# A decoder layer on one Trainium2 core: one unit's operand splits placed elsewhere, and seven steps of the passage to the feed-forward part reordered

## The chip, the cores and the metric

The kernel runs on one core of one Trainium2 chip. A core has five engines that run their own instruction streams side by side: TensorE (PE in the profile; its weight loads are PEld), VectorE (DVE), ScalarE (ACT), GpSimd (POOL) and SyncE (SP, which here only issues transfers). The metric is the device time of one execution in microseconds (us); smaller is better. The kernel before was run three times: 1386.6, 1388.0 and 1388.14 us, median 1388.0.

## What is computed

A post-norm decoder layer over 8 sequences of 256 tokens of 512 features (2048 tokens, 16 tiles of 128): a causal self-attention with 16 heads of 128 and rotary positions, a cross-attention with 16 heads of 32 over a context of the same size, and a feed-forward part of 2048 features with both products quantized (inputs to 8 bits per token, weights to three values). Cut to what matters:

```python
# self-attention: 16 heads x 128, rotary q and k, causal (masked scores are 0, not -inf)
scores = where(causal, q @ k.T / sqrt(128), 0)
m = max(abs(scores)); sgn = sign(scores)
attn_w = sgn * exp(sgn * scores - m)
attn = attn_w / (sum(abs(attn_w)) + 1e-6)
x = layernorm(x + (attn @ v) @ W_O + b_O)
# cross-attention, its result scaled and normalized
probs = softmax(clip(where(mask, q2 @ k2.T / sqrt(32), -1e4), -50, 50))
delta = rs * ((probs @ v2) @ Wo.T + bo)
x = layernorm(x + (delta - mean) / sqrt(var + EPS) * ln_gamma + ln_beta)
# feed-forward: bitlinear(x, w, b) = quant8(x) @ ternary(w).T + b
scale = 127 / max(abs(x), EPS)          # per token, in quant8
h = layernorm(gelu(bitlinear(x, w1, b1))) * gamma + beta
x = layernorm(x + bitlinear(h, w2, b2))
```

## The kernel before, in words

**Self-attention.** The work is cut into 32 units: 8 pairs of heads (hp) by 4 pairs of sequences (bp), the sequences inside. A unit projects q, k and v, turns q and k by the rotary tables, makes scores, exponentials, transposed weights, the product with v and the output projection. Most products need more than one pass: an fp32 operand is split into a high part (hi, a cast to fp32r) and the rest (lo), and `mm3` (L145 to L148) adds hi·hi (L146), hi·lo (L147) and lo·hi (L148). So whatever TensorE reads is split first: a cast and a subtraction, in `split` (L155 to L157) both at once, in `half_split` (L181 to L187) one at a time: L185 is the cast on ScalarE, L183 the subtraction. Units with hp 0 split their own input `xt` from two loaded halves (`raw`, three buffers). Unit 2's first half is split by `xsplit(0)`, its second by two calls of `x_half`; `xload` issues the two loads of a unit.

The order within a unit is a string of two- and three-letter words, `SCHED["unit"]` (L60 to L71). A word is a method with its indices: Q projects, s scores, a takes their magnitude and sign (L385, L386), S masks, m takes the maximum (L397, L398), x exponentials (L406), n the sum's reciprocal (L411, L412), N multiplies weight, reciprocal and sign into e (L419), t transposes e on TensorE (L426), c and k split it (L432, L433, L439), z multiplies with v (L146 to L148, L449), y and l split the result (L453, L458), o projects it (`ppo`). For q and k: w swaps halves (L314, L315), u multiplies with the cosine (L320), r with the sine (L324 on POOL), R adds (L330, L332 on POOL), H casts to hi (L341), L subtracts (L347 and L348). A unit's projections run interleaved with the attention of the unit before and the output projection of the one before that. Words such as X0, XA, XB, BY, G1 and BW are places at which `background` (L522 to L611) puts extra pieces: the next unit's splits, loads, and weights. For unit 1, whose neighbours have little to interleave, the string is altered by a list of replacements (L633 to L637). ScalarE, VectorE, POOL and SP are held to the order written; TensorE's order in these units is left to the framework's scheduler.

**The rest** (cross-attention, the quantized inputs, the feed-forward part) is written as steps `S(...)` (L686) with the tiles that they read and write. A planner (L1234 to L1348) simulates the engines, picks by priorities from a table (`PLAN`), and writes the steps into the list `done`; where a step may run on two engines, a string in `PLAN` says which. The steps are then emitted in the order of `done`, and all five engines are held to that order.

For each of the 16 token tiles, unit ("x", b) ends with the second norm and the quantized input of the feed-forward part: `rstd` (L764, L765 on POOL) makes the reciprocal deviation, L980 the normalized row, `absmax` (L985 to L987) the quantization scale, `inverse` (L992 to L1001, POOL) the factor `a1s` and three bf16 pieces of the reciprocal, put into `xq[:, 512:640]` beside the quantized values (L1004, L1008). L1006 adds the bias b2 to the row, on POOL or VectorE. SP then transposes `xq` (L1010) and stores it (L1011). A feed-forward tile f loads it (L1060), multiplies with the first weights (L1070, L1071), Gelu on ScalarE (L1075), mean (L1080), squares (L1084, ScalarE), `spread` (L1089 to L1091, POOL), the norm with gamma and beta in two halves (L1095, L1108 on VectorE for one; L1103 on ScalarE, L1105 on VectorE and L1107 on POOL for the other), the maximum (L1111), the scale (L1116 to L1118; L1121 on POOL), the quantization (L1124 on ScalarE, L1125 on VectorE), SP's transposing transfer of `hq` to `hT` (L1153), the second product (L1131, L1133), the sum (L1155), the last norm (L753, L754, L764, L765, L768) and its row y (L1161), and the store (L1162). SP issues its transfers one after the other, in order, and waits at each for its source.

Of the kernel before, what the change touches and what calls it, by code (L numbers as in the profile page):

```python
# [11 lines left out]
F32R = mybir.dt.float32r  # L12
# [4 lines left out]
ALU = mybir.AluOpType  # L17
AX = mybir.AxisListType

B, S, D = 8, 256, 512  # L20
# [4 lines left out]
NT = NTOK // 128  # L25
# [7 lines left out]
EPS = 1e-5  # L33
# [45 lines left out]
def decoder_kernel(ctx: ExitStack, tc: tile.TileContext, a, out):  # L79
    nc = tc.nc  # L80
# [27 lines left out]
    def T(tag, shape, dt=F32, name=None):  # L108
        return (keep if tag in ("w", "xt") else sb).tile(shape, dt, name=name or tag, tag=tag, bufs=BUFS.get(tag, 1))
# [66 lines left out]
    def x_half(t, raw, i, part, eng):  # L176
        tf = t.rearrange("p h k c -> p h (k c)")
        cs = slice(1024 * i, 1024 * i + 1024)
        half_split(tf[:, 0, cs], tf[:, 1, cs], raw, part, eng)
# [342 lines left out]
    def background(ui):  # L522
        u = units[ui]
        ex = {k: [] for k in ("B0", "BA", "BV", "BW", "BX", "BY", "XA", "XB", "X0", "X1", "G0", "G1", "BP", "WK", "WV")}
        if ui == 0:
            ex["WK"].append(lambda: load_first("wK"))
            ex["WV"].append(lambda: load_hp(0, "wV", first["wV"]))
        nx = units[ui + 1] if ui + 1 < len(units) else None
        if nx is not None and nx.hp == 0:
            if ui == 0:  # L530
                ex["BA"].append(nx.xload)
            ex["X0" if ui < 2 else "B0"].append(lambda: nx.xsplit(0))
            ex["XA"].append(lambda: x_half(nx.xt, nx.raws[1], 1, 0, nc.scalar))
            ex["XB" if ui > 1 else "X1"].append(lambda: x_half(nx.xt, nx.raws[1], 1, 1, nc.vector))
        elif nx is not None:
            ex["BA"].append(nx.load)
        if ui < 2:
            ex["BV" if ui else "BW"].append(units[ui + 2].xload)
        if u.hp == 0:
            ex["BA" if ui else "X1"].append(lambda: init_acc(u.bp))  # L540
            ex["BA" if ui else "X1"].append(lambda: nc.sync.dma_start(f32(xs[u.bp][:]), f32(u.xt[:])))
        if "wv" in late:
            ex["B0"].append(lambda raw=late.pop("wv"): load_hp(u.hp, "wV", raw["w"]))
        for n, hp, k1 in ([("wO", u.hp, "BW")] if ui else [], [] if ui > 1 else [("wO", 0, "BW")], [("wQ", u.hp + 1, "BW")], [("wK", u.hp + 1, ""), ("wV", u.hp + 1, "")])[u.bp]:
            if (ui or n == "wO") and hp < NHP:
                raws = {}
                ex["BV" if n == "wV" else "BA"].append(lambda n=n, hp=hp, raws=raws: raws.update(w=raw_load(a[n][hp])))
                if n == "wV":
                    late["wv"] = raws
                elif n == "wK":  # L550
                    def hi(raws=raws, hp=hp):
                        w = hw.setdefault(hp, {})["wK"] = T("w", [128, 2, 1024], F32R)
                        half_split(w[:, 0], w[:, 1], raws["w"], 0, nc.scalar)

                    def lo(raws=raws, hp=hp):
                        w = hw[hp]["wK"]
                        half_split(w[:, 0], w[:, 1], raws["w"], 1, nc.vector)

                    ex["G0"].append(hi)
                    ex["BX"].append(lo)  # L560
                else:
                    ex[k1].append(lambda n=n, hp=hp, raws=raws: load_hp(hp, n, raws["w"]))
        if ui in ABS:
            for j in range(2):
                i, rr = 2 * ABS.index(ui) + j, {}
                ex["BA"].append(lambda i=i, rr=rr: rr.update(w=wchunk(i // 8, i % 8)))
                ex[f"G{j}"].append(lambda i=i, rr=rr: wq_abs(rr["w"], i // 8, i % 8))
        if "r2" in late:
            ex["B0"].append(lambda f=late.pop("r2"): run(f))
        for n, ci in enumerate(ROUND.get(ui, ())):  # L570
            cr = {}
            ex["BV" if n else "BA"].append(lambda cr=cr, ci=ci: cr.update(w=wchunk(ci // 8, ci % 8)))
            fs = [lambda step=step, cr=cr, ci=ci: wq_round(cr["w"], ci // 8, ci % 8, step) for step in range(3)]
            if n:
                late["r2"] = fs
            else:
                for k, f in zip(("G0", "G1", "BW"), fs):
                    ex[k].append(f)
        if ui == 1:
            ex["BA"].append(lambda: bo.update(t=bcast("bc", "bO")))  # L580
        if ui == len(units) - 2:
            ex["BA"].append(lambda: kv0.update(wk0r=raw_load(a["wkx"][:, 0:1024])))
            ex["BW"].append(lambda: kv0.update(wk0=split_w(kv0["wk0r"])))
        if ui == len(units) - 1:
            ex["BA"].append(lambda: kv0.update(cr=x_raws(a["ctxT"][0])))

            def ctx_split(i):
                if i == 0:
                    kv0["ctx"] = T("xt", [128, 2, 4, 512], F32R)
                x_split(kv0["ctx"], kv0["cr"][i], i, (nc.vector, nc.gpsimd)[i])  # L590

            ex["X0"].append(lambda: ctx_split(0))
            ex["X0"].append(lambda: kv0.update(wk1r=raw_load(a["wkx"][:, 1024:2048])))

            def last(part, e):
                if part == 0:
                    kv0["wk1"] = T("w", [128, 2, 1024], F32R)
                x_half(kv0["ctx"], kv0["cr"][1], 1, part, e)
                half_split(kv0["wk1"][:, 0], kv0["wk1"][:, 1], kv0["wk1r"], part, e)

            ex["G0"].append(lambda: last(0, nc.scalar))
            ex["BW"].append(lambda: last(1, nc.vector))
        if ui == 4:
            ex["BA"].append(setup_late)
        if ui == 5:
            ex["G0"].append(setup_late2)
        if ui in (A0 + 8, A0 + 9):
            ex["G0"] += [lambda wi=wi: (wq_tot, wq_mean)[ui - A0 - 8](wi) for wi in range(2)]
        if A0 + 2 <= ui < A0 + 18:
            ex["BP"].append(lambda: add_bo(ui - A0 - 2))  # L610
        return ex  # L611
# [19 lines left out]
    for ui, u in enumerate(units):  # L631
        spec = SCHED["unit" if ui else "first"]
        if ui == 1:  # L633
            for old, new in ((" N0 XB", ""), (" n0 m1", " n0 N0 m1"), ("Q000 s00 Q001", "Q000 Q001 s00"), (" S0 BA", " S0 BA f0- f2-"),
                             (" V0 v0", ""), (" t00", " V0 v0 t00")):
                assert old in spec
                spec = spec.replace(old, new, 1)  # L637
        emit(spec, u, units[ui - 1] if ui > 0 else None, units[ui - 2] if ui > 1 else None, background(ui))
        if ui == 0:
            in_order(["PE", "Activation", "DVE", "Pool", "SP"])  # L640
# [120 lines left out]
        nc.scalar.activation(mv[:, 1:2], mv[:, 6:7], AF.Identity, scale=1.0 / D)  # L761

    def rstd(mv):
        nc.gpsimd.tensor_scalar(mv[:, 2:3], mv[:, 1:2], EPS, None, ALU.add)  # L764
        nc.gpsimd.tensor_tensor(mv[:, 3:4], mv[:, 2:3], nhalf, ALU.pow)  # L765

    def shift(mv):
# [86 lines left out]
    def x(b):  # L854
# [80 lines left out]
        for qi in range(2):  # L935
# [29 lines left out]
            def scale1(m1=m1):  # L965
# [9 lines left out]
              rd=[m1, A], wr=[d])  # L975
            S([("DVE", 0.8, lambda d=d, m2=m2: stats(H[d], H[m2])),
               ("ACT", 2.1, lambda d=d, m2=m2, xq=xq: astats(H[d], H[m2], H[xq][:, 0:512]))], rd=[d], wr=[m2, f"{xq}/q"], new=[m2] + new(xq))
            S([("POOL-", 1.0, lambda m2=m2: rstd(H[m2]))], wr=[m2])
            S([("DVE", 0.13, lambda m2=m2: shift(H[m2]))], wr=[m2])
            S([("ACT", 0.71, lambda tt=tt, d=d, m2=m2: nc.scalar.activation(acc[:, tt], H[d], AF.Identity, bias=H[m2][:, 2:3], scale=H[m2][:, 3:4]))],  # L980
              rd=[d, m2], wr=[A])
# [8 lines left out]

            def inverse(tt=tt, m2=m2, xq=xq):
                s, xq = H[m2], H[xq]  # L992
                nc.gpsimd.tensor_tensor(a1s[:, tt : tt + 1], s[:, 10:11], wscale[:, 0:1], ALU.mult)
                nc.gpsimd.memset(xq[:, 512:640], 0.0)
                inv = s[:, 12:13]
                nc.gpsimd.tensor_tensor(inv, s[:, 11:12], wscale[:, 2:3], ALU.mult)
                for n in (3, 2, 1):
                    c0 = 512 + 33 * (3 - n)
                    nc.gpsimd.tensor_copy(xq[:, c0 : c0 + 32 * n - 31 : 32], inv.to_broadcast([128, n]))
                    if n > 1:  # L1000
                        nc.gpsimd.tensor_tensor(inv, inv, xq[:, c0 : c0 + 1], ALU.subtract)  # L1001
# [293 lines left out]
    while pool_:  # L1295
# [47 lines left out]
        for t in succ[s]:  # L1343
            need[t] -= 1
            ready[t] = max(ready[t], end + LAG[s.eng] if s in t.deps else now)
            if need[t] == 0:
                insort(pool_, t, key=lambda s: (s.prio, s.i))
    assert len(done) == len(steps)  # L1348
    for s in done:
        for k in s.new:  # L1350
            g = place[k]
            p = px[g] if g in px else keep if g in ("w", "xt") else post
            H[k] = p.tile(tiles[k][1], tiles[k][2], name=k, tag=g, bufs=CAP[g])
        s.fn()
# [70 lines left out]
```

## Time and profile before

| | |
|---|---|
| median of three runs | 1388.0 us |
| profiled execution | 1387.89 us |
| its span, first to last instruction | 1386.1 us |
| around the span | 1.8 us |
| granted TensorE clock, mean | 0.992 |
| TensorE busy | 1346.7 us (97%) |
| VectorE busy | 1091.8 us (79%) |
| ScalarE busy | 880.4 us (64%) |
| POOL busy | 782.0 us (56%) |

Times in the profile are microseconds from the start of the span. A row names the line of the kernel, the operation, the tile written and those read. `xt` is a unit's split input, `raw` a loaded piece, `u` the rotated operand, `rh` its split parts, `ppj` a projection in PSUM, `pwt` transposed weights, `ppo` the output projection; `xq`, `xT` and `xqs` the quantized input, its transpose and its place in DRAM; `up` and `dn` the two feed-forward products, `h` the hidden row, `fs` its statistics, `hq` and `hT` its quantized form and that one's transpose, `mb` the statistics of the second norm and `my` those of the last. Self-attention ends at about 905 us, cross-attention at about 1230; the feed-forward part overlaps its end and runs on to 1386. A row's duration includes what the instruction waits for inside the engine, so the same instruction can show different durations.

In the waits, the columns after the colon are us in total, times, and the longest. In the chain of waits they are start, duration and what it was. In the timeline they are start, duration, engine, line, operation, tiles and shapes; idle time before an instruction and what ended it stand in brackets.

### The profile page before, as it was taken

What the parts mean: (1) busy time and instruction counts of PE and PEld (TensorE: products, weight loads), DVE (VectorE), ACT (ScalarE), POOL (GpSimd) and SP (SyncE); (2) the same over time, 40 slices, a digit from 0 to 9 for tenths busy, and PEclk for the clock granted to TensorE, in tenths of its full rate; (3) what the DMA queues carried; (4) which work ended last, traced back from release to release, by engine and by line L of the source; (5) the groups of instructions that cost most, each with busy time, mean ns of one, the idle gap of its engine ahead of it and who ended that gap; (6) DMA issues with size and microseconds to landing.
All of it is one profiled execution on the core that took longest, in us unless ns stands there. A gap on an engine that the chain in (4) does not pass through costs nothing.

```text
span 1386.1 us, 23778 instructions
## 1 busy us (share of the span) xinstructions
PE 1346.7 (97%) x8576; PEld 1081.0 (78%) x8576; DVE 1091.8 (79%) x2040; ACT 880.4 (64%) x1948; POOL 782.0 (56%) x985
## 2 busy tenths in 40 slices
PE   9899999999999999999999999999999999988896
PEld 7789988898889888998889888888667667543342
DVE  6877768778767888887877876868767877798997
ACT  4666776776776666666665666633644445576995
POOL 5656556656666666766665665525033324376764
PEclk9999999999999999999999999999999999999999
DMA  8442342234322244223422342225324424214453
GB/s 309 182 185 109 116 178 107 92 114 165 121 76 96 92 143 176 104 84 124 189 88 99 126 175 107 69 99 191 114 59 126 140 68 143 86 34 94 113 116 99
DMA packets 85046, 170.13 MB, mean 123 GB/s; under 512 B 47040, under 2 KB 57024, under 8 KB 80064
## 3 DMA queue, kind: packets, MB, share of 16 engines
q1 hardware_dynamic: 82624, 165.99, 35.1%
q10 hardware_dynamic: 2304, 2.62, 0.7%
q8 instruction: 68, 1.11, 0.3%
q14 instruction: 50, 0.41, 0.1%
HBM read 130.31 MB, written 27.79 MB: 114 GB/s over the span
## 4 chain that ended last, share of the span: by engine, by line
PE 82%; DVE 10%; POOL 3%; ACT 2%; issue 2%; DMA 1%; SPq 0%; POOLq 0%; ACTq 0%; DVEq 0%
PE ppj L146 12%; PE ppj L147 12%; PE ppj L148 12%; PE pz L146 3%; PE pz L148 3%; PE pz L147 3%; PE pwt L426 3%; PE sc L880 3%; PE den L911 2%; PE av L895 2%; PE ppo L146 2%; PE ppo L147 2%; PE ppo L148 2%; PE psc L376 2%; PE pz L449 2%
## 5 line engine op out<-in xcount | busy, mean ns | idle before, releaser
L324 POOL TENSOR_TENSOR sw<-sw,stab 128x512 f32<-128x512 f32 x128 | 170.2, 1329 | 101.5 <-ACT sw L315 101.0
L146 PE MATMUL ppj<-xt,w 128*128 128x512 f32 x528 | 209.0, 396 | 0.3 <-ACT xt L285 0.3
L147 PE MATMUL ppj<-xt,w 128*128 128x512 f32 x528 | 206.5, 391 | 1.0 <-DVE xt L157 0.4
L148 PE MATMUL ppj<-xt,w 128*128 128x512 f32 x528 | 206.2, 391 | 0.0
L146 PE MATMUL ppj<-w,xt 128*128 128x256 f32 (+1 forms) x528 | 157.2, 298 | 1.1 <-DVE u L320 1.1
L348 POOL TENSOR_TENSOR rh<-u,rh 128x512 fp32r<-128x512 f32 x64 | 97.6, 1526 | 99.8 <-PE ppj L148 88.2
L148 PE MATMUL ppj<-w,xt 128*128 128x256 f32 (+1 forms) x528 | 152.0, 288 | 0.0
L147 PE MATMUL ppj<-w,xt 128*128 128x256 f32 (+1 forms) x528 | 151.9, 288 | 0.0
L320 DVE SCALAR_TENSOR_TENSOR u<-ppj,bqk,ctab 128x512 f32<-128x512 f32 x128 | 95.5, 746 | 70.9 <-ACT sw L315 70.6
L314 ACT ACTIVATE sw<-ppj,bqk 64x512 f32<-64x512 f32 x128 | 87.8, 686 | 92.7 <-PE ppj L148 87.9
L332 POOL TENSOR_TENSOR u<-u,sw 128x256 f32<-128x256 f32 (+1 forms) x128 | 130.8, 1022 | 0.3 <-DVE u L320 0.2
L419 DVE SCALAR_TENSOR_TENSOR e<-aw,rd,sg 128x128 f32<-128x128 f32 (+1 forms) x256 | 126.3, 550 | 0.1
L148 PEld LDWEIGHTS ppj<-xt,w 128*128 128x128 f32 x528 | 99.2, 188 | 21.6 <-DVE w L183 0.4
L406 ACT ACTIVATE aw<-aw,nm 128x256 f32<-128x256 f32 (+1 forms) x256 | 113.2, 443 | 3.9 <-DVE nm L397 3.9
L391 POOL TENSOR_SCALAR_AFFINE_SELECT aw<-aw 128x256 f32<-128x256 f32 x128 | 59.9, 492 | 98.7 <-ACT aw L385 98.7
L453 ACT CAST z<-pz 128x512 fp32r<-128x512 f32 x64 | 37.6, 587 | 121.3 <-PE pz L449 121.3
L147 PEld LDWEIGHTS ppj<-xt,w 128*128 128x128 f32 x528 | 99.3, 188 | 17.9 <-DVE xt L183 0.8
L146 PEld LDWEIGHTS ppj<-xt,w 128*128 128x128 f32 x528 | 99.3, 188 | 17.1 <-ACT xt L285 0.7
L146 PEld LDWEIGHTS ppj<-w,xt 128*128 128x128 f32 x528 | 101.9, 193 | 2.0 <-DVE u L320 1.4
L147 PEld LDWEIGHTS ppj<-w,xt 128*128 128x128 f32 x528 | 102.0, 193 | 0.6
L148 PEld LDWEIGHTS ppj<-w,xt 128*128 128x128 f32 x528 | 101.7, 193 | 0.7
L385 ACT ACTIVATE aw<-psc 128x384 f32<-128x384 f32 x128 | 62.3, 487 | 60.6 <-PE psc L148 59.9
(283 smaller groups left out, 3937.0 us busy)
## 6 DMA issues: line engine op xcount, KB each, us to landing
xt<-xs SPq DMA_DIRECT2D x28, 2048.0 KB, 8.2
xs<-xt SPq DMA_DIRECT2D x4, 2048.0 KB, 12.9
raw<-w1T SPq DMA_DIRECT2D x16, 512.0 KB, 9.5
raw<-w2T SPq DMA_DIRECT2D x16, 512.0 KB, 9.6
acc<-xn SPq DMA_DIRECT2D x4, 1024.0 KB, 8.5
raw<-wO SPq DMA_DIRECT2D x8, 512.0 KB, 9.6
wq<-wqt SPq DMA_DIRECT2D x16, 256.0 KB, 2.4
kx<-ks SPq DMA_DIRECT2D x8, 512.0 KB, 4.9
```

The costliest lines, as they stand in the source:

```text
L146: nc.tensor.matmul(ps, lh, rh, start=first, stop=False)
L147: nc.tensor.matmul(ps, lh, rl, start=False, stop=False)
L148: nc.tensor.matmul(ps, ll, rh, start=False, stop=last)
L314: nc.scalar.activation(sw[0:64], ps[64:128], AF.Identity, bias=bias[64:128])
L320: nc.vector.scalar_tensor_tensor(v3(u), v3(self.ps.pop((h, i))), self.bias(h, i), ctab.to_broadcast([128, 2, 256]), ALU.add, ALU.mult)
L324: nc.gpsimd.tensor_tensor(v3(sw), v3(sw), stab.to_broadcast([128, 2, 256]), ALU.mult)
L332: nc.gpsimd.tensor_tensor(u, u, sw, ALU.add)
L348: (nc.gpsimd if i else nc.vector).tensor_tensor(lo, u if i else u[:, :, 128:256], f32(hi), ALU.subtract)
L385: nc.scalar.activation(aw[:, h], sc3, AF.Abs, scale=1.0 / math.sqrt(DH))
L391: nc.gpsimd.affine_select(aw[:, :, blk], aw[:, :, blk], pattern=[[0, 2], [-1, 128]], compare_op=ALU.is_ge, fill=MASKED, base=0, channel_mu ...
L406: nc.scalar.activation(aw[:, h, blk], aw[:, h, blk], AF.Exp, bias=nm[:, h, i : i + 1], accum_out=rd[:, h, i : i + 1])
L419: nc.vector.scalar_tensor_tensor(e[:, h, blk], aw[:, h, blk], rd[:, h, i : i + 1], sg[:, h, blk], ALU.mult, ALU.mult)
```

## The change

**Unit 1.** The first half of unit 2's input is split after the second block's e (`N1 X0`), not after the first block's maxima. Its second half's hi (ScalarE, `XA`) comes just before `l0`, its lo (VectorE) at `BY`. The first block's sum and e (`n0 N0`) come right before the second half of the key's `L00`, `u10` and `m1`; `x0` comes before `H00`. The weight wO of the first head pair is split in two steps, hi on ScalarE at `G1` and lo on VectorE at `BW`, where it was cast and subtracted on VectorE at `BW`.

**rstd** multiplies by 1.0 and adds EPS in one instruction, where it added EPS alone.

**inverse** makes `a1s` and the reciprocal for tiles 0 to 14 by one product of two columns, the reciprocal in the next column of `a1s`; the last tile keeps two products. The memset of `xq[:, 512:640]` moves to the step of the second norm's `rstd`.

**Seven steps** are moved by hand in `done` after the planner: hT0's transfer ahead of the transposition of xT14; tile 3's squares (L1084) ahead of tile 2's first quantization (L1124); behind both beta products (L1107) of tiles 2 and 1, and ahead of L1121 of tile 0, in this order: tile 3's `spread`, the last tile's `inverse`, and the last L1006, which also goes from VectorE to POOL; and xT15's transposition and store behind the first output store, ahead of hT3's transfer. SP's order was: xT14, xT15, their two stores, hT0, hT1, hT2, the first output, hT3. It is: hT0, xT14, its store, hT1, hT2, the first output, xT15, its store, hT3.

```diff
@@ background @@
-            ex["XB" if ui > 1 else "X1"].append(lambda: x_half(nx.xt, nx.raws[1], 1, 1, nc.vector))
+            ex["XB" if ui > 1 else "BY" if ui else "X1"].append(lambda: x_half(nx.xt, nx.raws[1], 1, 1, nc.vector))
...
-                elif n == "wK":
-                    def hi(raws=raws, hp=hp):
-                        w = hw.setdefault(hp, {})["wK"] = T("w", [128, 2, 1024], F32R)
+                elif n == "wK" or ui == 1:
+                    def hi(raws=raws, hp=hp, n=n):
+                        w = hw.setdefault(hp, {})[n] = T("w", [128, 2, 1024], F32R)
                         half_split(w[:, 0], w[:, 1], raws["w"], 0, nc.scalar)
...
-                    ex["G0"].append(hi)
-                    ex["BX"].append(lo)
+                    ex["G0" if n == "wK" else "G1"].append(hi)
+                    ex["BX" if n == "wK" else "BW"].append(lo)
@@ the order of unit 1 @@
-            for old, new in ((" N0 XB", ""), (" n0 m1", " n0 N0 m1"), ("Q000 s00 Q001", "Q000 Q001 s00"), (" S0 BA", " S0 BA f0- f2-"),
+            for old, new in ((" N0 XB", ""), (" L00 n0 m1", " n0 N0 L00 u10 m1"), (" H01 u10 R10", " H01 R10"), (" H00 x0 a11 XA", " x0 H00 a11"), (" R00 X0", " R00"), (" N1 X1", " N1 X0"),
+                             (" l0 k10 k11 BX", " XA l0 k10 k11 BX"), ("Q000 s00 Q001", "Q000 Q001 s00"), (" S0 BA", " S0 BA f0- f2-"),
@@ rstd @@
-        nc.gpsimd.tensor_scalar(mv[:, 2:3], mv[:, 1:2], EPS, None, ALU.add)
+        nc.gpsimd.tensor_scalar(mv[:, 2:3], mv[:, 1:2], 1.0, EPS, ALU.mult, ALU.add)
@@ the second norm's rstd, and inverse @@
-            S([("POOL-", 1.0, lambda m2=m2: rstd(H[m2]))], wr=[m2])
+            def rstd_zero(m2=m2, xq=xq):
+                rstd(H[m2])
+                nc.gpsimd.memset(H[xq][:, 512:640], 0.0)
+
+            S([("POOL-", 1.0, rstd_zero)], wr=[m2])
...
-                nc.gpsimd.tensor_tensor(a1s[:, tt : tt + 1], s[:, 10:11], wscale[:, 0:1], ALU.mult)
-                nc.gpsimd.memset(xq[:, 512:640], 0.0)
-                inv = s[:, 12:13]
-                nc.gpsimd.tensor_tensor(inv, s[:, 11:12], wscale[:, 2:3], ALU.mult)
+                if tt < NT - 1:
+                    inv = a1s[:, tt + 1 : tt + 2]
+                    nc.gpsimd.tensor_tensor(a1s[:, tt : tt + 2], s[:, 10:12], wscale[:, 0:4:2], ALU.mult)
+                else:
+                    inv = s[:, 12:13]
+                    nc.gpsimd.tensor_tensor(a1s[:, tt : tt + 1], s[:, 10:11], wscale[:, 0:1], ALU.mult)
+                    nc.gpsimd.tensor_tensor(inv, s[:, 11:12], wscale[:, 2:3], ALU.mult)
@@ behind the planner @@
+    at = {(*s.unit, s.label[1]): s for s in done}
+    for a_, b_ in (
+        (("f", 0, 19), ("x", 7, 58)),
+        (("f", 3, 6), ("f", 1, 12)),
+        (("f", 3, 7), ("f", 0, 16)),
+        (("x", 7, 72), ("f", 0, 16)),
+        (("x", 7, 74), ("f", 0, 16)),
+        (("x", 7, 76), ("f", 3, 19)),
+        (("x", 7, 77), ("f", 3, 19)),
+    ):
+        done.remove(at[a_])
+        done.insert(done.index(at[b_]), at[a_])
+    at["x", 7, 74].fn = at["x", 7, 74].opts[0][2]
```

## Prediction

> **What bounds the kernel.** I read the engine busy times by stretch first, then who waits for whom in the two stretches that the edits touch, then the chain of waits behind the second, last the rows of each engine there. By stretch (the columns are start:end, us of the stretch, busy us and instructions of PE, PEld, DVE, ACT and POOL, the granted TensorE clock, the DMA share, GB/s):
>
> ```profile
> 40.00:50.00 10.00, 6.17 (x33) 4.96 (x32) 7.31 (x15) 9.04 (x25) 7.62 (x10) 0.84 0.17 55
> 50.00:60.00 10.00, 10.00 (x67) 9.69 (x67) 8.40 (x16) 3.94 (x14) 5.12 (x5) 0.82 0.27 66
> 960.00:1220.00 260.00, 258.89 (x2267) 176.60 (x2266) 194.97 (x357) 135.50 (x188) 89.33 (x199) 1.00 0.34 104
> 1240.00:1260.00 20.00, 13.67 (x58) 5.48 (x57) 15.93 (x33) 12.90 (x18) 16.11 (x27) 0.93 0.34 75
> 1300.00:1340.00 40.00, 37.74 (x174) 16.68 (x172) 39.42 (x72) 38.41 (x48) 27.40 (x35) 1.00 0.55 117
> ```
>
> TensorE sets the time nearly to 1220: 258.89 of 260 us busy. Behind it VectorE (39.42 of 40) and ScalarE (38.41 of 40) set it together. Two places fall out: 40 to 50, with TensorE busy 6.17 of 10 us, and 1240 to 1260, where no engine is full. POOL has 260 - 89 = 171 us to spare in the cross-attention. In the first place, who waited for what between 20 and 110:
>
> ```profile
> PE pwt L426 <- DVE e L419: 2.6, 3, 1.6
> PE ppj L146 <- DVE u L320: 1.1, 1, 1.1
> ```
>
> That is 3.7 us, all for VectorE. VectorE's rows show what it did instead:
>
> ```profile
> 36.40 0.86 DVE L156 CAST xt<-raw 128x1024 fp32r<-128x1024 f32 x1
> 37.30 2.20 DVE L157 TENSOR_TENSOR xt<-raw,xt 128x1024 fp32r<-128x1024 f32 x1
> 39.42 0.74 DVE L320 SCALAR_TENSOR_TENSOR u<-ppj,bqk,ctab 128x512 f32<-128x512 f32 x1
> ```
>
> The split of unit 2's input, not needed before 57.4, stands ahead of u (L320); then come POOL's L332 to 40.8, ScalarE's cast (idle 3.13 us before it) and exponentials (41.13 to 43.0), then e (43.45 to 46.2). In the second place the chain of waits reads:
>
> ```profile
> 1247.98 1.27 POOL a1s L993
> ...
> 1250.39 1.19 POOL mb L1001
> ...
> 1252.38 2.57 DMA xT<-xq
> 1254.97 0.32 SPq L1011
> 1255.39 4.32 DMA hT<-hq
> 1259.75 6.37 PE dn L1131 x16
> ```
>
> The last tile's reciprocal on POOL (L993 to L999) holds up its transposing transfer, and SP, in order, holds hT0's behind that, though hq0 was ready at 1238.9 (L1124, L1125). From 1266 on the chain is VectorE's, and its and ScalarE's large waits here are
>
> ```profile
> DVE fs L1111 <- POOL h L1107: 3.0, 1, 3.0
> ACT hq L1124 <- POOL fs L1121: 6.1, 1, 6.1
> ```
>
> The beta products (L1107, 4.65 us for two) are behind the same reciprocal on POOL. ScalarE's 6.1 us follow from it: VectorE's maximum of h2 feeds the scale (L1118, ended 1257.5), then L1124 at 1257.59.
>
> **The early part, about -1.0 us.** Nothing is removed; unit 1's order changes. The first half's split goes behind the second block's e, its second half's hi later on ScalarE and lo later on VectorE, and wO's hi moves to ScalarE. Without L156, the exponentials can start when ScalarE's swap ends, at 37.7 for 41.13; e, 2.34 us when unhindered (52.60), ends near 42.4 for 46.2, in time for the transposes. Then u frees TensorE near 44.3 for 47.84: 3.6 us. The half clock, which the trace has from 46.75 to 53.57, costs 10 x 0.16 + 10 x 0.18 = 3.4 us of TensorE's work by the two rows. The most is 7.0 us. I take much less, because the delayed split falls due: the second e ended at 54.94 and can come about 1.4 us sooner, behind POOL's lo part of rh (L348) at 48.1 for 50.6. The split behind it takes 0.68 + 1.31 = 2.0 us (as the next one at 63.18), so it ends near 55.7: the product that needs it starts at 55.7 for 57.41. The second half's lo (1.21 us, behind two L458 and L439) frees its product at 59.1 for 59.95, the next scores come at 60.75 for 61.40, the output projection's L147 at 64.4 for 65.51. The four are 1.7, 0.85, 0.65 and 1.1 us ahead; I take 1.0, from 0 to 3.0 at the likeliest. From there TensorE is full, so it stays. SP's part: unit 3's x load (39.52) waits for the delayed split to free its buffer. At 55.7, landing in 3.8 to 7.3 us as these loads do, it is there at 59.5 to 63.0; VectorE wants it near 62. The second half's load, acc's and the store of x go from 56.2 to 59.1.
>
> **The late part, about -2.5 us.** On SP hT0's transfer goes ahead of xT14's, so from 1255.39 to about 1239; it lands near 1243.3 (4.32 us). TensorE's first down product then runs after the up products end (1254.98), not at 1259.75: its 4.77 us idle goes. That itself is cover only: y0 (L1155) sits at 1266.72 behind other VectorE work. What is late next is VectorE. On POOL the 4.3 us of the last reciprocal go behind both L1107, whose first can start when h2's gamma product ends at 1249.2. It takes 2.37 us (1265.68): L1111 can follow at about 1251.7, 3.0 us sooner, or, with h1's L1108 (1.25 us) waiting in between for POOL, at 1253.1, 1.6 us sooner. That they do block each other the rows show: L1107 took 3.33 us at 1272.88, begun under L1108, and L1116 2.19 us at 1274.04 for 0.15, begun under L1107. I take 1.6. Beyond it: L1006 leaves VectorE (0.67 us, in the stretch already idle); the waits for POOL's fs3 (0.46) and, since the squares of tile 3 run on ScalarE at 1251.45 instead of 1258.73, for h3 (0.24) go, and part of h4's 0.86. That is 1.6 + 0.46 + 0.24 = 2.3 and up to 3.2. Against it L1006, 1.25 us on POOL (1246.75), can block a VectorE instruction for as long. Between 1.05 and 4.6 (3.04 + 0.46 + 0.24 + 0.86) I take 2.5.
>
> On SP xT15's transposition (1.2 us to issue, 2.57 to land) and store go between the first output store and hT3's transfer. hT3 then comes about 0.4 us sooner than 1279.74 where all else is 2.5 sooner, so the fourth down product waits about 2 us more. Its y (1294.30) has 6 us of slack behind the product's end at 1287.9; the tile that xT15 feeds is last. Price nothing; without the slack, 2 us.
>
> **The rest, 0.** Each of 15 reciprocals loses one POOL product (L996, 0.30 us), its memset (L994, 0.2 us) moves ahead, into the step after the second norm, and the added EPS gets a multiplication. No row has L764 in that form; the nearest, L1089 (multiply, add: 0.27 us) and L764 itself (0.32 to 0.38), give ±0.1 for each of 32. POOL's 171 us of spare hide the 16 of the cross-attention; of the output norm's 16, ScalarE waited for one (0.8 us at 1288.88), the others lie beside other work. In the transition the two memsets cost POOL 0.4 us, a product under a VectorE lock (L996, 1.08 us at 1243.41) goes. Bounds -0.7 to +0.4, taken 0.
>
> The profiled execution took 1387.9 us (span 1386.1, 1.8 around it), the median is 1388.0. **1387.9 - 1.0 - 2.5 + 0 = 1384.4 us.**
>
> [...]
>
> **Rivals.**
> 1. More goes than I take. Early, the clock stays up and the delayed split is no limit: up to 7.0, say 4.0. Late, L1107 and L1108 don't meet: 3.0 + 0.46 + 0.24 + 0.86 = 4.6 less some of L1006, 3.5. Time 1387.9 - 7.5 = 1380.4. For it: the rows of 40 to 60 do hold that loss. Against: VectorE is 84% busy from 50 to 60.
> 2. No net change. POOL gets the second L1107 before h1's L1108: L1108 runs 1254.1 to 1255.4, VectorE's next maxima at 1255.4, 0.7 later than now, and the 0.46 + 0.24 + 0.86 that go leave a late gain of about 0.9; the early one is given back at the delayed split (0). Time 1387.0. [...]
> 3. Slower, by one mechanism: the delayed split of unit 2's input. If the second e is not earlier than today, the split (0.86 + 2.20 us under a POOL lock, as at 36.40) ends at 58.0, 0.6 after TensorE wants it, and unit 3's load, issued only then, lands at 61.8 to 65.3, so VectorE, in order, stands before that split up to 3 us, and u, e and TensorE behind it; one more half-clock stretch, 3.41 us long as from 1227.76 to 1231.17, costs 1.7. That is +5.3; with the late gain at 2.3, 1387.9 + 3.0 = 1390.9, at worst 1393. It decides if the split ends after about 57.4.
> 4. The reorder does not act, that is, the queues still wait elsewhere: 1387.9. The order of instructions on SP, POOL and ScalarE shows that it is as described; next to nothing.
>
> **How the numbers follow.** A measurement here tells 0.2%, 2.8 us, from no change: faster is below 1385.2, slower above 1390.8. The forecast with its own range (early 0 to 3.0, late 1.05 to 4.6, so 1380.3 to 1386.9) has 0.64, rival 1 0.16, rivals 2 and 4 0.12, rival 3 0.08. Of the forecast's 0.64, I put 0.50 below 1385.2, nearer its middle than its end. So faster 0.50 + 0.16 = 0.66, same 0.14 + 0.12 = 0.26, slower 0.08. The range runs from 1380.0, which takes in half of rival 1, to 1388.4, past rivals 2 and 4; outside are 0.08 + 0.08 and a little of the sum's own spread.
>
> **What would show it.** Right: TensorE's waits for e (L419) and u (L320) between 40 and 50 gone; the product on unit 2's first half near 55.7; hT0's transfer issued near 1239 and the first down product without a wait behind the up products; L1111 of h2 near 1252 (after the shift by 1.0); ScalarE's 6.1 us idle before L1124 cut by the 2.2 us of squares. Wrong: a VectorE wait for raw near 62, the half clock still on after 47, L1108 or L1116 of a microsecond more beside L1107 or L1006, a wait of ScalarE for hT3's transfer. An early gain lost before 960 would show that VectorE or SP, not TensorE, paced some unit.

## The result, and the profile after

The changed kernel takes 1384.63 us (median of 12 runs, 1383.86 to 1386.57) beside 1387.16 us before (12 runs, 1386.56 to 1388.47). The ratio is 0.9982 (95% interval 0.9975 to 0.9989): 2.5 us less, between 1.5 and 3.5. The profiled execution took 1384.0 us with a span of 1382.1.

In the changed kernel the numbers of the feed-forward's lines are 8 higher: L1103 is the gamma product that was L1095, L1111 the ScalarE step that was L1103, L1113 the product that was L1105, L1115 the beta product (L1107), L1116 the other half's (L1108), L1119 the maximum (L1111), L1014 the bias (L1006), L1161 hT's transfer (L1153). L765 and L766 are rstd.

By stretch, the columns as before:

```profile
40.00:50.00 10.00, 7.09 (x49) 5.75 (x47) 7.31 (x15) 6.45 (x19) 7.35 (x9) 1.00 0.01 2
50.00:60.00 10.00, 8.80 (x55) 7.11 (x54) 9.97 (x19) 6.17 (x15) 4.21 (x5) 1.00 0.18 62
1240.00:1260.00 20.00, 18.34 (x80) 7.62 (x80) 19.59 (x32) 16.30 (x22) 16.93 (x25) 0.97 0.31 71
1300.00:1340.00 40.00, 38.41 (x177) 17.17 (x178) 39.45 (x70) 38.43 (x47) 26.20 (x35) 1.00 0.52 115
```

The half clock between 40 and 60 is gone in this execution (1.00 in both rows), but TensorE is now busy only 8.80 of 10 us from 50 to 60, and VectorE 9.97: the stall was pushed 10 us on, and VectorE is what it waits for. Over the whole passage TensorE idles no less than before, 26 - 21.89 = 4.11 us for 26 - 22.17 = 3.83 (the row before, then the row after):

```profile
40.00:66.00 26.00, 22.17 (x128) 19.40 (x127) 21.64 (x38) 17.95 (x48) 16.28 (x18) 0.87 0.40 140
```

```profile
40.00:66.00 26.00, 21.89 (x132) 17.84 (x131) 22.50 (x41) 17.16 (x40) 16.70 (x18) 1.00 0.30 99
```

From 1240 to 1260 VectorE went from 15.93 to 19.59 of 20 us, so its hole is closed. TensorE's waits from 20 to 110, after:

```profile
PE pwt L426 <- DVE e L419: 1.3, 2, 0.8
PE ppj L146 <- DVE u L320: 1.1, 2, 0.6
PE ppj L147 <- DVE xt L157: 1.0, 2, 0.6
PE psc L147 <- POOL rh L348: 0.9, 1, 0.9
```

The first two were 2.6 and 1.1; the third, 1.0 us for the split that was moved, was 0.4. In VectorE's rows the split now stands here:

```profile
53.64 0.68 DVE L156 CAST xt<-raw 128x1024 fp32r<-128x1024 f32 x1
54.35 1.22 DVE L157 TENSOR_TENSOR xt<-raw,xt 128x1024 fp32r<-128x1024 f32 x1
```

In the transition, rows of POOL from the timeline (start in us, duration, and in brackets a wait and what ended it):

```profile
1246.78 5.76 POOL L1115 TENSOR_TENSOR h<-h,be 128x1024 f32<-128x1024 f32 x2 [1.26 <-DVE h L1113]
1256.13 1.78 POOL L1014 TENSOR_TENSOR acc<-acc,b2b 128x512 f32<-128x512 f32 x1
```

and VectorE's beside them:

```profile
1247.03 3.30 DVE L1116 SCALAR_TENSOR_TENSOR h<-h,fs,be 128x1024 f32<-128x1024 f32 x1
...
1256.71 2.29 DVE L1103 SCALAR_TENSOR_TENSOR h<-h,fs,g 128x1024 f32<-128x1024 f32 x1
```

The two beta products began 5.5 us earlier than at 1252.31 (2.5 of it the lead that everything has at 1246). VectorE's L1116 came between them and took 3.30 us for 1.28. It ended 1.1 us behind the first product (2.46 us), and the second (3.34 us) ended 2.2 us behind it; together they took 5.76 us, for two of 2.37. They took turns, as in the traces of "inverse moves", "L1006 on VectorE" and "four more" below, where the same instruction takes 3.30, 3.30 and 3.31 us. L1103 took 2.29 us beside L1014.

To tell where the time went, the start of the same instruction is compared with the kernel before (us, from both traces; the row's time is that of the kernel before). The four parts of the next section stand beside it:

```
instruction            at    changed   unit 1   7 moves  POOL    hT0
first swap, L314       12    -0.70     -0.43    -0.25    -0.24   -0.11
swap, L314            119    -1.64     -1.41    -0.39    -0.43   -0.09
swap, L314            851    -1.72     -1.48    -0.45    -0.44   -0.15
absmax, tile 12      1220    -1.67     -1.83    -0.65    -0.89   -0.45
absmax, tile 15      1246    -2.50     -2.39    -0.66    -1.70   -0.45
gamma product, tile 3 1264   -4.05     -2.38    -2.42    -1.82   -0.44
gamma product, tile 5 1283   -4.61     -2.38    -2.43    -2.36   -0.44
gamma product, tile 6 1292   -4.01     -2.35    -2.43    -2.36   -0.45
last sum, L1155      1380    -4.03     -1.49    -1.60    -1.60   -0.45
```

The first row comes before any changed instruction: the two executions start 0.70 us apart. Then 0.94 are gained by 119, in unit 1, 0.83 between 1220 and 1246, 1.55 at the moved reciprocal, 0.56 near 1281, and 0.60 are lost before 1292. Without the 0.70 that is 3.3 us, of which the medians show 2.5. The table has a noise of its own: from 851 to 1220, where the parts change little or nothing, the traces differ from the kernel before by anything from 0.05 us more to 0.46 less (hT0 alone: 0.30 less). So a gain of a few tenths is believed only where the rows that make it are seen.

### The profile page after: what moved, and what is told of

It is laid out like the page before. It is cut to its first block, busy times and chain, and to the rows that moved or that the text cites. A ratio compares the mean times of both kernels' runs of the same rounds, so it can differ in the third digit from the quotient of the medians.

```text
span 1382.1 us, 23761 instructions
## 1 busy us (share of the span) xinstructions
PE 1342.4 (97%) x8564; PEld 1077.6 (78%) x8576; DVE 1091.2 (79%) x2038; ACT 881.6 (64%) x1949; POOL 777.0 (56%) x971
## 4 chain that ended last, share of the span: by engine, by line
PE 80%; DVE 12%; ACT 3%; issue 2%; POOL 2%; DMA 1%; SPq 0%; POOLq 0%; ACTq 0%; DVEq 0%
PE ppj L147 12%; PE ppj L146 12%; PE ppj L148 12%; PE pz L146 3%; PE pz L148 3%; PE pz L147 3%; PE pwt L426 3%; PE sc L881 3%; PE den L912 2%; PE av L896 2%; PE ppo L146 2%; PE ppo L147 2%; PE ppo L148 2%; PE psc L376 2%; PE pz L449 2%
## 5 line engine op out<-in xcount | busy, mean ns | idle before, releaser
L146 PEld LDWEIGHTS ppj<-w,xt 128*128 128x128 f32 x528 | 100.7, 191 | 2.4 <-DVE u L320 0.8
L147 PEld LDWEIGHTS ppj<-w,xt 128*128 128x128 f32 x528 | 100.9, 191 | 0.6
L148 PEld LDWEIGHTS ppj<-w,xt 128*128 128x128 f32 x528 | 100.7, 191 | 0.7
```

What stands on the lines that cost most here:

```text
L146: nc.tensor.matmul(ps, lh, rh, start=first, stop=False)
L147: nc.tensor.matmul(ps, lh, rl, start=False, stop=False)
L148: nc.tensor.matmul(ps, ll, rh, start=False, stop=last)
```

## The experiments

**Each part alone.**

```diff
# unit 1: the edits of background and of unit 1's string, nothing else
# 7 moves: the block behind the planner, nothing else
# POOL: rstd, rstd_zero and inverse, nothing else
# hT0: of the block, one line
+        (("f", 0, 19), ("x", 7, 58)),
```

> Only unit 1's new order and the two-step split of wO; the reciprocals, rstd and the seven moved steps stay as before. Theory (the early gain is VectorE's split out of the way, limited by the same split falling due later): 1.0 us less than before, all of it gained between 35 and 66 us and kept to the end, with TensorE waiting for xt (L157) near 55. Rival (the early gain is the half clock that is avoided): 2 to 3.4 us less. Rival (TensorE catches up elsewhere, nothing is kept): 0.

> Only the seven moved steps, with L1006 of the last tile on POOL; unit 1, rstd and inverse as before. Theory: 1.6 to 2.3 us less, all of it gained between the last inverse and the gamma product of tile 3 (L1105, 1264 us before). If the shorter inverse is what helps in the transition, this gives less than 1.

> Only rstd in its new form, the reciprocals with one product fewer and the memset moved. Theory (POOL has room, the term is 0): within 0.3 us of before. [...]

> Only hT0's transfer is moved ahead of xT14's; the other six steps, unit 1 and POOL's reciprocals as before. Theory (TensorE's 4.77 us idle before the first down product is cover, VectorE sets the end): within 0.3 us of before, though the idle and the half clock behind it go. Rival (the chain of waits through hT0's transfer and the first down product sets the end): 2 us or more less.

Measured beside 33 runs of the kernel before (1387.26 us), 11 runs each: unit 1 1386.70 us, ratio 0.9997 (0.9988 to 1.0005); seven moves 1385.62, 0.9989 (0.9980 to 0.9998); POOL 1386.10, 0.9989 (0.9980 to 0.9998); hT0 1386.84, 0.9998 (0.9989 to 1.0006). So unit 1 alone and hT0 alone are not told from no change by time; the other two are just told. The table is finer. The seven moves gain 1.76 between 1246 and 1264. hT0 alone gains nothing (0.11 at the start, 0.45 from the cross-attention on, which it does not touch).

Unit 1 gains 0.98 between 12 and 119 and keeps it to 1220, the size that the theory had. What it is gained from shows when the time between these two swaps is put side by side for all traces, the later ones too:

```
order of unit 1               traces  half clock in it                12 to 119, us
old                           4       6.8 us, from 46.0 to 46.8 on    107.07 to 107.28
old ("inverse moves", below)  1       6.8 us, from 43.88 on           106.33
new                           4       none                            106.29 to 106.35
new                           2       3.4 us, from 46.2 or 46.5 on    106.28 and 106.32
new, hi on ScalarE (below)    3       none in two, 3.4 us in one      106.09 to 106.11
```

In the new order the half clock costs nothing; the delayed split sets the time, as the theory had it (in all six traces the product that needs it starts 44.2 to 44.3 us behind the first swap), and a shorter split on VectorE takes 0.2 us off. In the old order the half clock makes the difference. In the fifth trace of the old order TensorE still waits for e and u:

```profile
PE pwt L426 <- DVE e L419: 2.4, 3, 1.6
PE ppj L146 <- DVE u L320: 0.9, 1, 0.9
```

But the half clock begins about 2 us sooner in the kernel's course, so that more of it falls on these waits and less on the full stretch behind them (3.6 us for 5.7 in the kernel before), and this execution of the old order is as fast as the new one. So the new order moves TensorE's waits without shortening them, and what it gains on the old order is what the half clock costs there, 0 to 0.95 us by where it falls: the cause is the rival's, if less than its 2 to 3.4 us, the limit the theory's. How often it falls which way, five traces do not tell.

The POOL part was to give nothing and gives three things. The subtraction L952, whose cT TensorE's product waits for, takes 1.02 us instead of 1.27 (0.26). L1006 of POOL runs beside it: it ends 0.72 us behind L952's start in the kernel before and 0.46 in the changed kernel (L952 there 1.01 us), and L952 ends 0.55 us behind it in both. The half clock at 1227.76 does not come (0.55). In all nine traces with the short reciprocals L952 takes 1.0 us and that half clock stays away; of the five without them it comes in four, and unit 1 alone escapes it with L952 at 1.27, so by where it fell. And near 1281 the part gains 0.54, for which here are rstd's two rows of POOL for tile 1, before:

```profile
1280.49 0.22 POOL L764 TENSOR_SCALAR my<-my 128x1 f32<-128x1 f32 x1 [2.96 <-DVE fs L1116]
1280.79 1.65 POOL L765 TENSOR_TENSOR my<-my,nhalf 128x1 f32<-128x1 f32 x1
```

and with the POOL part alone:

```profile
1278.66 0.19 POOL L764 TENSOR_SCALAR my<-my 128x1 f32<-128x1 f32 x1 [2.96 <-DVE fs L1123]
1278.94 0.55 POOL L765 TENSOR_TENSOR my<-my,nhalf 128x1 f32<-128x1 f32 x1
```

With the multiplication by 1.0 L764 is 0.03 us shorter (0.19 for 0.22). So L765 starts 0.02 us behind VectorE's gamma product (1278.92) and not 0.04 behind (1280.75); it takes 0.55 us, not 1.65, and VectorE's shift (L768) no longer waits 0.46 us for it. It is the same in all 14 traces: 1.65 us in the five with the old form, 0.55 in the nine with the new one.

All of the three parts lose 0.75 to 0.86 us in the last row. That is the clock; see below.

**Which of the seven moves.**

```diff
# "inverse moves": the kernel before with four of the seven
-        (("f", 0, 19), ("x", 7, 58)),
-        (("f", 3, 6), ("f", 1, 12)),
-        (("f", 3, 7), ("f", 0, 16)),
# "hT0 behind xT14": the changed kernel with one line taken out
-        (("f", 0, 19), ("x", 7, 58)),
```

> Of the seven moves only four: the last reciprocal and the last L1006 (on POOL) behind both beta products, and xT15's transposition and store behind the first output store. hT0's transfer, tile 3's squares and its spread stay where they were; unit 1, rstd and inverse as before. All seven gained 1.77 us between the products of 1246 and L1105 of tile 3. Theory (the beta products were waiting for the reciprocal; the squares save the waits of 0.46 and 0.24 us): 1.1 to 1.4 us of these remain. Rival (it is the squares and the spread of tile 3, done early, that save ScalarE's 6 us): less than 0.5 remains.

> The changed kernel without the first of the seven moves: hT0's transfer stands behind xT14's transposition and store, the rest is as changed. Theory (that move is cover only, as it was alone): the sums of tile 0 and all behind them within 0.2 us of the changed kernel. Rival (the move is what lets the others keep their gain, and without it the later transfers and hT3 slip): 0.5 to 1.4 us later from tile 3 on.

Each is read from the trace of one execution. The four moves gain 1.44 us by tile 3's gamma product, just above the theory's 1.1 to 1.4, but only 0.08 are left at tile 6. In between stands this row of ScalarE, tile 6's squares:

```profile
1284.21 2.00 ACT L1084 ACTIVATE hq<-h,fs 128x2048 bf16<-128x2048 f32 x1 [2.30 <-DMA hT<-hq]
```

It writes into the buffer that hT3's transfer reads, so it waits for that transfer, which SP issues behind xT15's (1275.55, 2.10 us to issue) and its store. So the moved xT15 has a price. The seven moves do not pay it (2.43 at tiles 5 and 6, with a wait of 1.44 us there). Whether tile 3's squares and spread, or hT0, make up for it was only half told apart: without hT0's move the changed kernel runs as before that (0.35 us ahead at 1220 and at 1264, 0.25 ahead at 1292). So hT0's move is cover, as predicted, and it is not what keeps the gain. How much of it the squares keep was not tried alone.

**What the changed kernel still loses.**

```diff
# "L1006 on VectorE"
-    at["x", 7, 74].fn = at["x", 7, 74].opts[0][2]
# "spread 4 first"
+        (("f", 3, 11), ("f", 4, 8)),
# "hi on ScalarE": unit 2's first half in two steps
+                def hi0():
+                    nx.xt = T("xt", [128, 2, 4, 512], F32R)
+                    x_half(nx.xt, nx.raws[0], 0, 0, nc.scalar)
+                ex["X1"].append(hi0)
+                ex["X0"].append(lambda: x_half(nx.xt, nx.raws[0], 0, 1, nc.vector))
...
-                             (" N1 X1", " N1 X0")
+                             (" N1 X1 f0", " N1 f0 X1 X0")
```

> The changed kernel with the last L1006 back on VectorE, behind the same steps. [...]

> The changed kernel with one more move: tile 4's spread on POOL ahead of tile 3's beta product, where ScalarE waited 5.82 us for it and VectorE 0.86 us behind that. Theory: the 0.86 us go, so from L1113 of tile 4 on everything is 0.5 to 0.9 us sooner against the changed kernel. Rival (VectorE's work as such sets the pace, or L1111 of tile 3 then waits for the later beta product): within 0.2 us.

> The changed kernel with the cast of unit 2's first half on ScalarE, in its idle time of 2.7 us near 51, instead of on VectorE. Theory (the early gain is limited by VectorE's delayed split, for which TensorE waits 1.0 us in L147): VectorE saves 0.68 us, the split ends 0.4 to 0.7 us sooner and the units from 90 us on run 0.3 to 0.7 us sooner against the changed kernel, measured from the first swap at 12 us. Rival (another chain, POOL's or ScalarE's, sets unit 1): within 0.15 us.

Each is read from one execution, against the changed kernel's trace. With L1006 on VectorE, L1103 is back at

```profile
1257.20 1.28 DVE L1103 SCALAR_TENSOR_TENSOR h<-h,fs,g 128x1024 f32<-128x1024 f32 x1
```

and tile 3's gamma product comes 0.43 us sooner (0.11 at 1246, 0.54 at 1260). So the last L1006 on POOL costs 1.0 us on L1103 to save 0.67. With tile 4's spread first, ScalarE's wait for it is 2.13 us; it was 5.82 in the changed kernel, whose row comes second:

```profile
1262.55 1.24 ACT L1111 ACTIVATE h<-h,fs 128x1024 f32<-128x1024 f32 x1 [2.13 <-POOL fs L1099]
```

```profile
1266.23 1.24 ACT L1111 ACTIVATE h<-h,fs 128x1024 f32<-128x1024 f32 x1 [5.82 <-POOL fs L1099]
```

The gain is 0.55 us; 0.38 of the 0.86 go to a gamma product that meets POOL (L1103 1.64 us). The cast on ScalarE gains 0.21 us by 62, less than the theory's 0.3 and more than the rival's 0.15. TensorE's two waits show why:

```profile
PE ppj L147 <- DVE xt L183: 0.6, 2, 0.3
PE ppj L147 <- DVE xt L157: 0.4, 1, 0.4
```

L157's fell from 1.0 to 0.4, L183's rose from 0.3 to 0.6: the second half's split is next in VectorE's queue.

**The clock near the end, and the version that beats both.**

```diff
# "tail kept busy", in down()
+            if tt == 14:
+                for _ in range(11):
+                    nc.tensor.matmul(H[dn], H["fw1"][:, 0:128], H["fw1"][:, 0:512], start=True, stop=True)
# "four more": hi on ScalarE, spread 4 first, and
-        (("x", 7, 74), ("f", 0, 16)),
-        (("x", 7, 76), ("f", 3, 19)),
-        (("x", 7, 77), ("f", 3, 19)),
+        (("x", 7, 74), ("f", 14, 21)),
+        (("x", 7, 76), ("f", 5, 19)),
+        (("x", 7, 77), ("f", 5, 19)),
```

> The changed kernel with 11 products more on TensorE ahead of tile 14's second product, whose result that product overwrites: they fill the 2.9 us in which TensorE waits for hT14 near the end. Theory (in some executions, as in those of the three parts, this wait fills enough of one 3.41 us stretch for the clock to be halved; then tile 14's product takes 5.3 us instead of 3.6 and the end comes 0.8 to 1.2 us later): no half clock between 1360 and 1372, a profile within 0.2 us of the changed kernel's undisturbed end, and a median 0.2 to 0.8 us below the changed kernel's. Rival (the end is VectorE's, the half clock there costs nothing): the same median within 0.2 us.

> The changed kernel with four edits more: the cast of unit 2's first half on ScalarE (0.2 us in its trace), tile 4's spread ahead of tile 3's beta product (0.5), the last L1006 on POOL but only ahead of tile 14's sum, away from VectorE's full stretch (1.0, or 0.45 and 0.6), and xT15's transposition and store behind hT4's transfer, ahead of hT5's. Theory: ScalarE's wait of 1.4 us for hT3 goes, with it VectorE's 0.24 and 0.20; in all 1.5 to 2.2 us less than the changed kernel. Rival (VectorE then meets POOL's products elsewhere): 0.7 or less.

> The four edits and the 11 filling products together. Theory: the two gains add up, 1.9 to 2.8 us less than the changed kernel; against the kernel with the four edits alone, 0.2 to 0.8 us. Rival: no difference to the four edits alone.

TensorE's wait for hT14 is the same in all kernels without the filling (2.78 to 2.95 us), what follows is not. Unit 1 alone, then the changed kernel (L1132, L1139 and L1142 are the second product, L1131 before):

```profile
1367.12 5.31 PE L1132 MATMUL dn<-fw,hT 128*128 128x512 f16 x16 [2.93 <-DMA hT<-hq]
```

```profile
1365.40 3.63 PE L1139 MATMUL dn<-fw,hT 128*128 128x512 f16 x16 [2.91 <-DMA hT<-hq]
```

In the records of the granted clock all half-clock stretches of a trace begin and end on one grid of 3.413 us (to 0.003 us in all 14 traces, the trace's end aside). In the first trace 2.4 us of the wait lie in one cell of it (TensorE busy 0.30 of the cell), and the next cell has half clock; in the second the wait falls across two cells (busy 0.57 and 0.58), and none comes. With the filling products

```profile
1362.76 2.54 PE L1140 MATMUL dn<-fw 128*128 128x512 f16 x11
1365.87 3.63 PE L1142 MATMUL dn<-fw,hT 128*128 128x512 f16 x16 [0.57 <-DMA hT<-hq]
```

the wait is 0.57 us and the last sum keeps its place (0.46 behind the changed kernel at 1366, 0.47 at 1376). By time it is 1384.36 us, 0.9980 (0.9971 to 0.9989) of the kernel before, against 0.9982: the 0.3 us between the medians are not told from none.

Four edits more give 1382.67 us (5 runs, 1381.96 to 1383.13), 0.9965 (0.9951 to 0.9978); with the filling products 1382.18 (5 runs, 1382.07 to 1383.00), 0.9964 (0.9951 to 0.9976). That is 2.0 and 2.5 us less than the changed kernel's 1384.63, and 4.4 and 4.9 less than the kernel before in the same set (1387.05): faster than both. The trace of the four edits splits the gain: 1.03 us for L1006, 0.42 for the spread, and 0.60 for xT15 (the lead goes from 1.79 us at 1277 to 2.39 at 1288). hT3's transfer (L1169 there) is issued at

```profile
1273.88 1.94 SPq L1169 DMA_TRANSPOSE hT<-hq  x1
```

instead of 1277.97. The filling adds nothing that the times can tell. The trace without it met two half clocks more, 1.0 us lost behind a wait of 2.18 us for xx, a tile's loaded input, at 1335 and 0.5 at the end; the one with it met neither, and only the second is the filling's doing.

## Why the prediction was right

**The early part** was right in its limit, the delayed split, and in its size: 1.0 us predicted, 0.94 in the changed kernel, 0.98 alone. Part of that is luck. The split was put to end near 55.7 and ended at 55.57, the product behind it came at 55.63; but this execution ran 0.70 us ahead from its start. Counted from the first swap, that product came 1.07 us sooner and not 1.7. The steps ahead of it were too hopeful: e takes 3.69 us, not 2.34, with POOL at work beside it from 39.99 to 43.49; the second e ends 0.5 us sooner, not 1.4; TensorE's next projection starts 2.1 us sooner, not 3.6. The waits for e and u, whose going was named as a sign of being right, shrank from 3.7 us to 2.4 and came back elsewhere, 4.11 us of idle for 3.83. What was gained is the half clock alone, which the sum had among its 7.0 us and did not count by itself, and one trace of the old order has no such loss. Rival 3, unit 3's late load, did not come: SP issued it at 55.61, and VectorE split it at 60.83 without a wait.

**The reorder** was predicted at 2.5 us for the whole late part, 2.3 of it at the reciprocal and the two waits. It gave 1.55 there. Row by row, the maximum behind tile 2's beta product came 1.86 us sooner (1254.68 to 1250.32, less the lead of 2.50), for the 1.6 that was taken, and by the turn-taking that was chosen. The second rival, POOL running both products ahead of VectorE's beta product, is not what the trace shows: L1116 (3.30 us) ended 2.2 us before the second product did. The waits of 0.46 and 0.24 us did go. What failed is the rest of that term: L1006 on POOL took 1.0 us back, near its bound of 1.25, and h4's 0.86 stayed, because POOL takes tile 3's beta product before tile 4's spread. Two of the signs of being wrong came with this: L1116 2.0 us longer beside a beta product, and ScalarE's wait for hT3.

**"The rest, 0"** was wrong: 0.83 us between 1220 and 1246 and 0.56 near 1281, beyond the bound of 0.7 that was given. I looked at the cross-attention, where POOL's room does hide all (0.05 us lost between 851 and 1220 in the changed kernel), and not at the one VectorE step (L952) that meets L1006 at its end; and 0.03 us of an instruction decided whether L765 took 0.55 or 1.65 us. That difference stood in the rows before: where nothing holds them up, L1089 (multiply and add) takes 0.19 us and L764 0.22. The 0.27 and 0.32 to 0.38 of the prediction are means that hold waits.

**hT0's move** was right: cover, in the place where it was alone and in the full set. The half clock behind TensorE's idle time, which was to go with it, did not: the trace of hT0 alone has one from 1261.77 to 1272.01, at no cost. **xT15** was priced at nothing and cost 0.60 us: I followed TensorE's fourth product and its slack, not ScalarE's squares of tile 6, which need hT3's transfer too and waited 1.38 us for it. It costs that only where VectorE has run so far ahead: the seven moves alone wait 1.44 us and lose nothing, so the wait takes back what L765's 0.55 us for 1.65 near 1281 had given.

So the late 2.5 us came out at 2.34, by 1.55 + 0.83 + 0.56 - 0.60. That it is so near is luck: the reorder fell 0.95 short, and three terms that I had at 0 made up 0.79. The sum of both parts, 3.5 us, stands beside 3.3 in the trace and 2.5 in the medians. The remaining 0.8 is not settled. The two traced executions were not middling ones: 1387.89 us before is 0.73 above its median, 1384.0 after 0.63 below. A half clock near the end, as in the three parts, would fit as well: of the 12 runs the four with a mean granted clock of 0.993 or 0.994 took 1383.86 to 1384.15 us, the eight with 0.991 or 0.992 took 1384.43 to 1386.57. But the mean does not tell where a half clock lay, and only one of them has a trace, and it is one of the four.

## What to carry to other kernels

An edit that closes a hole is worth what the next one in the queue allows: before counting the stall, find where the displaced work falls due, and compare more than one execution of the kernel before: a clock that falls elsewhere can give the same gain without the edit (106.33 us from 12 to 119 in one trace of the old order, 106.28 to 106.35 in the new). A small operation moved to another engine "because it has room" may cost the busy one more than it saved: L1006 on POOL took 0.67 us off VectorE, and L1103 beside it took 1.0 us longer. For a transfer moved back in a queue, follow every reader of what now stands behind it, not only the one that the chain of waits names.

## What the runs showed of the hardware

In the 14 traces the granted clock of TensorE changed between full and half only on the grid of 3.413 us, which lay differently from execution to execution: before, half clock runs from 46.75 to 53.58 and from 1227.76 to 1231.17, in the changed kernel from 1234.26 to 1241.09 and from 1278.64 to 1285.46. In these traces every full-clock cell with TensorE busy 0.38 or less was followed by half clock (47 cells), and none with more than 0.57. Between them it went both ways, at 0.46 for instance (half clock behind 1224.35 before, none behind 1221.38 in unit 1 alone). The two of 0.57 (spread 4 first at 42.82, tail kept busy at 43.12) hold transposes of e (L426); without these they were busy 0.28. If transposes are left out everywhere, only cells from 0.37 to 0.46 go both ways. No run here tests the transposes by themselves. At half clock, 29 cells with up to 0.78 were followed by another at half clock, 47 with 0.82 and more by one at full clock. The wait of 1.85 us (before, ended at 1226.63) was followed by half clock, and the one of 2.91 us (changed, ended at 1365.40) was not.

The gains of the parts do not add up to the measured whole: near the end the wait for hT14 lay mostly in one cell in unit 1 alone and across two in the changed kernel, and between 1292 and 1380 the three parts lost 0.75 to 0.86 us each, the changed kernel nothing.
